# Paired context products, one claim for two turned weight tiles, and latents kept with all 128 rows

## The chip, the core and the metric

One core of a Trainium2 chip runs the whole kernel. Its engines work beside each other and meet at semaphores: PE (matrix multiply), DVE, ACT and POOL (element work), and SP, which here only issues DMAs. The time is the device time of one execution in microseconds; lower is better. The kernel before has a median of 1673.97 us over three runs (1671.38 to 1674.11). 0.2% of that, 3.3 us, is about what can be told from no change.

## What is computed

One post-norm decoder layer on 8 sequences of 256 tokens, 256 wide, all in float32:

```
x = layernorm(x + self_attention(x))
x = layernorm(x + cross_attention(x, ctx))
x = layernorm(x + mixture_of_experts(x))      # 8 experts, hidden 1024, all computed, 2 weighted
```

Self-attention has 16 heads and three branches that share the query and are mixed by a gate:

```
nq  = rms(x @ w_cq) * g_q          # 96 latent columns  -> queries
ckv = rms(x @ w_ckv) * g_kv        # 32 latent columns  -> keys and values of the latent branch
k_nope = ckv @ w_dk_nope ;  v1 = ckv @ w_dv
a1 = causal attention over the latent keys, a2 = over 64 selected tokens, a3 = causal over plain keys
out = (g0*a1 + g1*a2 + g2*a3) @ w_proj
```

Cross-attention has 16 heads of 16 columns over 256 context tokens. The experts' matrices make up most of the work.

## The kernel before

Every step is a Python generator ("thread") that yields operations. A planner, `Machine.run`, keeps a clock for each engine, picks among the threads' next operations by start time and rank, and so writes one fixed order of instructions for each engine. A low rank is preferred; the experts have rank 99 and fill what is left. A tile comes from a pool with a tag and a number of buffers; `m.claim` makes a thread wait until all the buffers it names are free, and reserves the short ones. The planner books a load as 0.6 us of issue, its bytes at 330 GB/s, one after the other, and 2.5 us to land (`commit`). None of this is visible on the chip except as the order of the instructions and the buffers that they share.

The work of a sequence `s` runs in units of four heads, `g` = 0 to 3:

- `raw` and `latents` make the 128 latent columns, 96 for the queries and 32 for keys and values. `latents` normalises the 96 in place and writes the 32 twice, side by side, into a tile `twice`. PE transposes both parts (tile `plt`), DVE scales them with the norm's gains into `lT` (rows 0 to 95) and `lk` (64 rows, the 32 rows twice).
- `latent_pairs` makes the latent keys (`kn`) and values (`vl`) for two units at a time from `lk` and the weights `wkv`. It uses 32 rows of the array for each unit, so that the two units' matmuls run beside each other on different rows. Each writes a PSUM tile of its own (`pkn`, `pvl`), which is copied out by itself.
- `project` makes queries and keys; `first` makes the scores (tile `s`, also on 32 rows each); `weighing` makes the softmax weights `pr` and `pl`.
- `products` multiplies weights by values. For this the weights must stand turned. For sequence 0, `turned` does it with PE transposes (tile `pt`) and copies. For all others the weights are parked in DRAM (`parking`: a DVE transpose and a DMA `pr<-pr`, `pl<-pl`) and loaded back in another order (DMAs `pa<-pr`, `pb<-pl`). `pa` has the tag `pt` with one buffer, `pb` the tag `pb` with one.
- `second`, `x_weighing` and `x_products` do the same for cross-attention: weights `prx`, parked and loaded as `xpt`, which also takes the one buffer of tag `pt`. In `x_products` two units share one PSUM tile `ox`: the first unit is loaded and multiplied, its buffer is given back, then the second is loaded and multiplied.
- `context` prepares keys and values of the context for all sequences at rank 60; its mask tile is `keep`. `selection` finds the 64 tokens with a row tile of tag `sc`, and `after` (the router) takes the same tag for `rT`.

A float32 matmul of 256 columns stands in the trace as two MATMUL records (two passes), and a transpose as one. The experts' tiles are `ph` (first matrix) and `py` (second).

The two lines that matter most for what follows are the products' claims:

```
for src, name, tag in (("pr", "pa", "pt"), ("pl", "pb", "pb")):
    h[name] = yield from turned(s, g, h[src], src, name, tag)
```

## Time and profile before

| | |
|---|---|
| median of three runs | 1673.97 us |
| the profiled execution, whole | 1674.96 us |
| its span, first to last instruction | 1673.2 us |
| PE busy in the span | 1609.5 us (96%) |
| DVE busy | 1158.9 us (69%) |
| ACT, POOL busy | 583.8 us, 599.7 us |
| mean granted clock of PE | 0.986 |
| DMA queue's share of the 16 engines | 57.6% |

Busy counts an engine from an instruction's start to its end. PE's matmuls overlap, so a record's mean duration (382 ns for `ph`) is longer than the distance between two starts; costs on PE are therefore read from starts. The times are from one execution, which took 1.0 us more than the median.

### The profile page before, as it was taken

To read this page: it belongs to the slowest core of one execution; us is meant where nothing else is said; L and a number is where in the kernel's file an instruction comes from. 1 tells how busy PE (TensorE), PEld (TensorE's weight loads), DVE (VectorE), ACT (ScalarE), POOL (GpSimd) and SP (SyncE) were. 2 spreads that over 40 slices of the span, in tenths; PEclk is the share of its full clock that TensorE was granted. 3 is DMA by queue.
4 is the path that set the end of the run, shared out by engine and by line. 5 is a ranking of instruction groups with operands and counts; after the bars stand their busy time and mean duration, and the time that the engine had idled before them with its cause. 6 is when DMAs were issued, how large, how long until landed. Compare 5 with 4: busy or idle time off the path is not lost.

```text
span 1673.2 us, 31920 instructions
## 1 busy us (share of the span) xinstructions
PE 1609.5 (96%) x12040; PEld 1320.2 (79%) x12040; DVE 1158.9 (69%) x2577; ACT 583.8 (35%) x2114; POOL 599.7 (36%) x795
## 2 busy tenths in 40 slices
PE   6899789999999999999999999999999999999998
PEld 4778568887887778888888688878888778888887
DVE  4968678678789874887678884688767774544333
ACT  2464543244435430434434341244435341220000
POOL 3665753253534430334235332243335332120000
PEclk8999899999999999999999999999999999999999
DMA  6311416378648675655746676566656777585552
GB/s 218 117 50 47 166 69 217 120 245 284 233 141 291 245 248 192 211 205 189 252 172 234 241 249 227 151 238 211 226 196 221 248 257 251 154 307 153 161 156 96
DMA packets 185657, 329.96 MB, mean 197 GB/s; under 512 B 13200, under 2 KB 105504, under 8 KB 178336
## 3 DMA queue, kind: packets, MB, share of 16 engines
q1 hardware_dynamic: 185504, 327.92, 57.6%
q8 instruction: 96, 1.57, 0.4%
q14 instruction: 57, 0.47, 0.1%
HBM read 237.70 MB, written 90.19 MB: 196 GB/s over the span
## 4 chain that ended last, share of the span: by engine, by line
PE 83%; issue 7%; DVE 4%; DMA 3%; POOL 1%; SPq 1%; ACT 0%; POOLq 0%; DVEq 0%; ACTq 0%
PE ph L280 23%; PE py L280 22%; PE s L280 9%; PE o L280 4%; PE pk L280 3%; PE pyo L280 3%; PE ox L280 2%; PE pv L280 2%; PE sx L280 2%; DMA xpt<-prx 1%; PE pkm L280 1%; PE pks L280 1%; PE pq L280 1%; PE pt L286 1%; PE pkr L280 1%
## 5 line engine op out<-in xcount | busy, mean ns | idle before, releaser
L280 PE MATMUL ph<-xT,w 128*128 128x256 f32 x2048 | 475.2, 382 | 3.8 <-DVE pl L98 2.6
L280 PE MATMUL py<-w,h 128*128 128x256 f32 x2048 | 471.5, 381 | 0.0
L280 PEld LDWEIGHTS ph<-xT,w 128*128 128x128 f32 x2048 | 383.8, 190 | 70.2 <-issue 16.7
L280 PEld LDWEIGHTS py<-w,h 128*128 128x128 f32 x2048 | 383.7, 190 | 59.7 <-issue 7.7
L98 ACT ACTIVATE h<-ph,b 128x256 f32<-128x256 f32 x227 | 107.5, 473 | 391.5 <-PE ph L280 340.0
L98 DVE TENSOR_SCALAR h<-ph,b 128x256 f32<-128x256 f32 x285 | 136.9, 482 | 112.5 <-PE ph L280 109.6
L98 DVE SCALAR_TENSOR_TENSOR xr<-py,rw,xr 128x256 f32<-128x256 f32 x128 | 61.2, 478 | 174.7 <-PE py L280 174.6
L98 POOL TENSOR_TENSOR prx<-prx,sumsx 128x512 f32<-128x512 f32 x128 | 130.6, 1051 | 118.8 <-DVE sumsx L98 73.2
L98 ACT ACTIVATE prx<-sx,nmx 128x256 f32<-128x256 f32 x256 | 117.0, 486 | 43.3 <-DVE nmx L98 41.9
L98 POOL TENSOR_TENSOR pr<-pr,wpr 128x256 f32<-128x256 f32 (+2 forms) x128 | 129.4, 1042 | 0.0
L98 POOL TENSOR_TENSOR rstd<-var,nhalf 128x2 f32<-128x2 f32 x24 | 17.4, 725 | 310.0 <-DVE var L98 309.9
L98 ACT ACTIVATE pl<-pl,nmpl 128x128 f32<-128x128 f32 (+1 forms) x256 | 113.1, 446 | 30.6 <-DVE nmpl L98 29.9
L98 POOL TENSOR_TENSOR kx<-turn 128x64 f32<-128x64 f32 (+1 forms) x128 | 65.3, 527 | 162.6 <-DVE turn L98 156.9
L98 ACT ACTIVATE pr<-pr,nmpr 128x128 f32<-128x128 f32 (+1 forms) x256 | 113.2, 447 | 0.0
L98 DVE TENSOR_TENSOR pr<-s,causal 128x256 f32<-128x256 f32 x128 | 74.6, 583 | 41.0 <-PE s L280 34.6
L280 PE MATMUL s<-kx,q 32*128 32x320 f32 (+1 forms) x1536 | 96.1, 390 | 0.3 <-POOL kx L98 0.3
L98 POOL TENSOR_TENSOR pl<-pl,wpl 128x512 f32<-128x512 f32 x64 | 93.1, 1475 | 2.7
L98 POOL TENSOR_TENSOR q<-turn 128x256 f32<-128x256 f32 x64 | 45.8, 735 | 134.1 <-DVE turn L98 130.8
L280 PEld LDWEIGHTS s<-kx,q 32*128 32x128 f32 x1536 | 71.2, 189 | 17.8 <-issue 7.1
L98 DVE TENSOR_REDUCE nmx<-sx 128x2 f32<-128x512 f32 x128 | 79.1, 678 | 8.5 <-PE sx L280 8.5
L98 DVE TENSOR_TENSOR pl<-s,causal 128x256 f32<-128x256 f32 x128 | 74.3, 581 | 12.6 <-PE s L280 8.6
L98 DVE TENSOR_REDUCE nmpr<-pr 128x4 f32<-128x256 f32 (+2 forms) x128 | 80.5, 673 | 0.0
(217 smaller groups left out, 2385.1 us busy)
## 6 DMA issues: line engine op xcount, KB each, us to landing
w<-in_W SPq DMA_DIRECT2D x256, 512.0 KB, 4.2
pr<-pr SPq DMA_DIRECT2D x28, 1024.0 KB, 4.1
pa<-pr SPq DMA_DIRECT2D x28, 1024.0 KB, 6.9
prx<-prx SPq DMA_DIRECT2D x28, 1024.0 KB, 5.2
xpt<-prx SPq DMA_DIRECT2D x28, 1024.0 KB, 6.5
pl<-pl SPq DMA_DIRECT2D x28, 768.0 KB, 4.9
pb<-pl SPq DMA_DIRECT2D x28, 768.0 KB, 7.2
xT<-in_xT SPq DMA_DIRECT2D x8, 256.0 KB
```

The lines of the kernel that those rows point to most:

```text
L98: return Op(self.name, us, outs, ins, lambda: getattr(self.engine, kind)(*args, **kw))
L280: lambda: nc.tensor.matmul(out, lhsT, rhs, start=start, stop=stop, skip_group_check=share > 1),
L286: return Op("PE", 0.11, [out], [in_], lambda: nc.tensor.transpose(out, in_, ident[:n, :n]), lag=0.17)
```

## The change

In words: `wkv` gets 128 rows, zero in rows 0 to 95, and is loaded by one DMA instead of four. The latents stay together: all 128 columns are normalised in place, transposed by two instructions instead of four, and scaled by one DVE instruction into `lT`; `twice`, `lk` and `gkv` go. `latent_pairs` uses all 128 rows, one matmul after the other, into one PSUM tile, which is copied out by one instruction. `turned` takes a list of one unit's two weights, or of two units' one weight, claims two buffers of the tag `pt` (which now has two) at once, and only then loads or transposes. `x_products` multiplies two units in one run. To make room, `sv` moves to the tag `turn`, and `keep` to the tag `sc`, which has one buffer.

```diff
-    wkv = fixed("wkv", [64, 2, 2, P])
-    gkv = fixed("gkv", [64, 1])
+    wkv = fixed("wkv", [P, 2 * H * VH])
...
-        for n in range(2):
-            yield dma(gkv[bass.ts(n, 32)], a["g_norm"][QL:P])
...
-        for n in range(2):
-            for v in range(2):
-                yield dma(wkv[bass.ts(n, 32), :, v], up[n, v])
+        yield dma(wkv[QL:P], a["w_up"][QL:P, 0 : 2 * H * VH])
...
     def zeros():
+        yield G.memset(wkv[0:QL], 0.0)
...
-    def turned(s, g, t, src, name, tag):
-        if by_dram(s):
-            yield seen("parked", src, s, g)
+    def turned(s, todo):
+        dst = []
+        for t, src, g in todo:
+            if by_dram(s):
+                yield seen("parked", src, s, g)
+            dst.append(two([P, t.shape[1]], "pt", "turned"))
+        yield m.claim(*dst)
+        for x, (t, src, g) in zip(dst, todo):
+            yield from turn_one(s, g, t, src, x)
+        return dst
...
-        sv = one([P, H * VH], "sv", "sv")
+        sv = two([P, H * VH], "turn", "sv")
...
-        plt = mtile([P, 2, T], "plt")
-        yield group([tr(plt[0:QL, 0, bass.ts(i, P)], lat[:, i, 0:QL]) for i in range(2)])
-        yield group([tr(plt[0:64, 1, bass.ts(i, P)], twice[:, i].rearrange("p n c -> p (n c)")) for i in range(2)])
-        m.release(lat, twice)
-        yield V.tensor_scalar(lT[0:QL], plt[0:QL, 0], gcol[0:QL], None, ALU.mult)
-        yield V.tensor_scalar(lk, plt[0:64, 1], gkv, None, ALU.mult)
+        plt = mtile([P, T], "plt")
+        yield group([tr(plt[:, bass.ts(i, P)], lat[:, i]) for i in range(2)])
+        m.release(lat)
+        yield V.tensor_scalar(lT, plt, gcol, None, ALU.mult)
...
-                ps = [mtile([P, T], "p" + name) for _ in range(2)]
...
-                        ops.append((p_, wkv[rows, g, 0], lk[rows]))
-                    else:
-                        ops += [(p_[:, bass.ts(i, P)], lk[rows, bass.ts(i, P)], wkv[rows, g, 1]) for i in range(2)]
...
-                yield group([mm(*op, share=2) for op in ops], 0.1)
-                for n, p_ in enumerate(ps):
-                    yield copied(t[:, n], p_)
+                p_ = mtile([P, 2, T], "p" + name)
+                if name == "kn":
+                    yield group([mm(p_[:, n], wkv[:, bass.ts(2 * g + n, P)], lT) for n in range(2)])
+                else:
+                    w = wkv[:, bass.ds(H * VH + 2 * P * g, 2 * P)]
+                    yield group([mm(p_[:, i], lT[:, bass.ts(i, P)], w) for i in range(2)])
+                yield copied(t, p_)
...
-                for src, name, tag in (("pr", "pa", "pt"), ("pl", "pb", "pb")):
-                    h[name] = yield from turned(s, g, h[src], src, name, tag)
+                h["pa"], h["pb"] = yield from turned(s, [(h[src], src, g) for src in ("pr", "pl")])
...
-            keep = one([P, T], "keep", "keep")
+            keep = one([P, T], "sc", "keep")
...
-                for n in range(2):
-                    pr = xa[s][g + n]["pr"]
-                    xt = yield from turned(s, g + n, pr, "prx", "xpt", "pt")
+                both = yield from turned(s, [(xa[s][g + n]["pr"], "prx", g + n) for n in range(2)])
+                xt = [parts_of(x, s).rearrange("p k h (q c) r -> p h c q k r", q=2) for x in both]
...
+                        for n in range(2)
+                        for c in range(2)
+                        for j in reversed(range(4))
...
+                m.release(*both)
```

More of the change, by code (lines that the diff above doesn't have):

```diff
@@ L404, in setup @@
         yield seen("staged", 0)
-        up = a["w_up"][QL:P, 0 : 2 * H * VH].rearrange("r (v g n c) -> n v r g c", v=2, n=2, c=P)
-        for n in range(2):
-            for v in range(2):
-                yield dma(wkv[bass.ts(n, 32), :, v], up[n, v])
+        yield dma(wkv[QL:P], a["w_up"][QL:P, 0 : 2 * H * VH])
         done.add("latent weights")
@@ L621, in parking, with turn_one @@
                 done.add(("parked", name, s, g))
-    def turned(s, g, t, src, name, tag):
-        if by_dram(s):
-            yield seen("parked", src, s, g)
+    def turned(s, todo):
[8 more added lines that the diff above has]
+        return dst
+    def turn_one(s, g, t, src, dst):
         n = t.shape[1] // (P * HG)
-        dst = one([P, HG * n * P], tag, name)
-        yield m.claim(dst)
         if by_dram(s):
@@ L643, in turned @@
             m.release(t)
-        return dst
     def weigh(t, f):
@@ L774, in latents @@
         lT = one([P, T], "lT", "lT")
-        lk = one([64, T], "lk", "lk")
-        yield m.claim(lT, lk)
+        yield m.claim(lT)
         yield seen("inputs")
-        twice = two([P, 2, 2, 32], "turn", "twice")
-        yield V.tensor_tensor(
-            lat[:, :, 0:QL], lat[:, :, 0:QL], rs[:, 0, :].unsqueeze(2).to_broadcast([P, 2, QL]), ALU.mult
-        )
-        yield V.tensor_tensor(
-            twice,
-            lat[:, :, QL:P].unsqueeze(2).to_broadcast([P, 2, 2, 32]),
-            rs[:, 1, :].unsqueeze(2).unsqueeze(3).to_broadcast([P, 2, 2, 32]),
-            ALU.mult,
-        )
-        plt = mtile([P, 2, T], "plt")
-        yield group([tr(plt[0:QL, 0, bass.ts(i, P)], lat[:, i, 0:QL]) for i in range(2)])
-        yield group([tr(plt[0:64, 1, bass.ts(i, P)], twice[:, i].rearrange("p n c -> p (n c)")) for i in range(2)])
-        m.release(lat, twice)
-        yield V.tensor_scalar(lT[0:QL], plt[0:QL, 0], gcol[0:QL], None, ALU.mult)
-        yield V.tensor_scalar(lk, plt[0:64, 1], gkv, None, ALU.mult)
+        for w, (lo, hi) in enumerate(parts):
+            yield V.tensor_tensor(
+                lat[:, :, lo:hi], lat[:, :, lo:hi], rs[:, w, :].unsqueeze(2).to_broadcast([P, 2, hi - lo]), ALU.mult
+            )
+        plt = mtile([P, T], "plt")
+        yield group([tr(plt[:, bass.ts(i, P)], lat[:, i]) for i in range(2)])
+        m.release(lat)
+        yield V.tensor_scalar(lT, plt, gcol, None, ALU.mult)
         m.release(plt)
-        d["lT"], d["lk"] = lT, lk
+        d["lT"] = lT
         done.add(("latent", s))
@@ L919, in project @@
                 m.release(pv)
-                if g == NHG - 1:
-                    m.release(d["lT"])
                 done.add(("values", s, g))
@@ L930, in latent_pairs @@
                 yield seen("heads", s, 2 * g)
-                lk = d["lk"]
+                lT = d["lT"]
                 t = one([P, 2, T], name, name)
                 d[name, g] = t
-                ps = [mtile([P, T], "p" + name) for _ in range(2)]
-                yield m.claim(t)
-                yield m.claim(*ps)
-                ops = []
-                for n, p_ in enumerate(ps):
-                    rows = bass.ts(n, 32)
-                    if name == "kn":
-                        ops.append((p_, wkv[rows, g, 0], lk[rows]))
-                    else:
-                        ops += [(p_[:, bass.ts(i, P)], lk[rows, bass.ts(i, P)], wkv[rows, g, 1]) for i in range(2)]
-                if name != "kn":
-                    ops = ops[0::2] + ops[1::2]
-                yield group([mm(*op, share=2) for op in ops], 0.1)
-                for n, p_ in enumerate(ps):
-                    yield copied(t[:, n], p_)
-                m.release(*ps)
+                p_ = mtile([P, 2, T], "p" + name)
[5 more added lines that the diff above has]
+                yield copied(t, p_)
+                m.release(p_)
                 done.add((name, s, g))
-                if name != "kn" and g == 1:
-                    yield seen("kn", s, 1)
-                    m.release(lk)
+            if name == "vl":
+                yield seen("kn", s, 1)
+                yield seen("values", s, NHG - 1)
+                m.release(lT)
     def scores(h, d, g, st, which):
@@ L1072, in products @@
                 yield seen("vl", s, g // 2)
-                vl = pro[s]["vl", g // 2][:, g % 2].rearrange("p (i c) -> p i c", i=2)
+                vl = pro[s]["vl", g // 2][:, :, bass.ts(g % 2, P)]
                 if g == 0:
@@ L1298, in x_products @@
                 o = mtile([P, T], "ox")
-                for n in range(2):
-                    pr = xa[s][g + n]["pr"]
-                    xt = yield from turned(s, g + n, pr, "prx", "xpt", "pt")
-                    turned_ = parts_of(xt, s).rearrange("p k h (q c) r -> p h c q k r", q=2)
-                    yield group(
-                        [
-                            mm(
-                                o[bass.ts(j, 32)],
-                                vx[:, c, HG * (g + n) + j, :],
-                                turned_[:, j, c],
-                                n == 0 and c == 0,
-                                n == 1 and c == 1,
-                                share=4,
-                            )
-                            for c in range(2)
-                            for j in reversed(range(4))
-                        ],
-                        0.3,
-                    )
-                    m.release(xt)
+                both = yield from turned(s, [(xa[s][g + n]["pr"], "prx", g + n) for n in range(2)])
+                xt = [parts_of(x, s).rearrange("p k h (q c) r -> p h c q k r", q=2) for x in both]
+                yield group(
+                    [
+                        mm(
+                            o[bass.ts(j, 32)],
+                            vx[:, c, HG * (g + n) + j, :],
+                            xt[n][:, j, c],
+                            n == 0 and c == 0,
+                            n == 1 and c == 1,
+                            share=4,
+                        )
+                        for n in range(2)
+                        for c in range(2)
+                        for j in reversed(range(4))
+                    ],
+                    0.3,
+                )
+                m.release(*both)
                 yield copied(oT[:, g // 2, :], o)
```

## The prediction

> **What bounds the kernel now.** I read the page's busy shares first, then the busy time by stretch, because a mean over the span hides where PE has no work:

> ```profile
> PE 1609.5 (96%) x12040; PEld 1320.2 (79%) x12040; DVE 1158.9 (69%) x2577; ACT 583.8 (35%) x2114; POOL 599.7 (36%) x795
> ```

> ```profile
> 0.00:250.00 250.00, 210.12 (x1884) 166.34 (x1884) 181.48 (x451) 118.53 (x418) 145.66 (x208) 0.92 0.33 111
> 250.00:1631.00 1381.00, 1363.86 (x9995) 1122.92 (x9995) 963.89 (x2095) 465.26 (x1696) 453.34 (x587) 1.00 0.63 216
> 1631.00:1673.20 42.20, 35.56 (x165) 30.97 (x163) 13.52 (x31) 0.00 (x0) 0.69 (x1) 0.98 0.30 99
> ```

> In each row the stretch is followed by its length and PE's busy time; the clock is third from the right. PE idles 39.9 us in the first 250, 17.1 in the next 1381 and 6.6 at the end, when the last layernorm leaves. The first `ph` starts at 250.09: until then no expert can fill PE's gaps, and the way from sequence 0 to its experts sets the pace. After it PE is the bound, and a microsecond off another engine buys nothing. So two things count: PE's own work, start to start, and the waits that the planner's order leaves on PE.

> **PE's work.** The unit comes from the chain of waits, where PE runs without a break; then three places of the timeline (start, duration, records):

> ```profile
> 1542.24 6.91 PE ph L280 x32
> ```

> ```profile
> 511.70 0.81 PE L280 MATMUL ph<-xT,w 128*128 128x256 f32 x3
> ...
> 512.44 0.70 PE L280 MATMUL pkn<-lk,wkv 32*128 32x256 f32 x4
> ...
> 513.07 1.13 PE L280 MATMUL ph<-xT,w 128*128 128x256 f32 x4
> ...
> 552.79 0.71 PE L280 MATMUL pvl<-wkv,lk 32*128 32x128 f32 x8
> 553.44 0.92 PE L280 MATMUL py<-w,h 128*128 128x256 f32 x3
> ...
> 1214.27 0.38 PE L286 MATMUL plt<-ident,lat 128*96 128x128 f32 x2
> 1214.49 1.89 PE L280 MATMUL py<-w,h 128*128 128x256 f32 x8
> ...
> 1510.67 0.81 PE L280 MATMUL ph<-xT,w 128*128 128x256 f32 x3
> 1511.41 1.07 PE L280 MATMUL ox<-xpt,vx 128*32 128x256 f32 x16
> 1512.41 0.92 PE L280 MATMUL ph<-xT,w 128*128 128x256 f32 x3
> ```

> A 256-column record on the full array takes 6.91 / 32 = 0.216 us.

> *Latent keys and values.* Three `ph` records from 511.70 should hand over at 512.35; `pkn` starts at 512.44, 0.09 late, as the array changes from full to 32 rows. It then holds PE for 0.63. Packed `pkn` costs 0.72. On the full array its four records of 256 columns cost 4 x 0.216 = 0.86: 0.14 more. `pvl` holds PE for 0.65 and, with 0.09 before it, costs 0.74; afterwards it too has four records of 256 columns: 0.13 more. Read group by group, 11 of the 16 `pkn` and 14 of the 16 `pvl` groups enter from full-array work like these. The other 7 stand beside work that is packed anyway and cost about 0.43 (`pkn` from 40.50 to 40.93); they lose about 0.45 each. Sum: 11 x 0.14 + 14 x 0.13 + 7 x 0.45 = **+6.5 us**. [...]

> *Transposes.* The two `plt` of a part hold PE for 0.22 (1214.27 to 1214.49). Four become two for each of 8 sequences: **-1.8 us**.

> *Context products.* A run of 16 `ox` records costs 1.00 and 0.09 on entry. The tile's view has the last record of this run starting at 1512.1, so a step inside is 0.69 / 15 = 0.046 us and the exit 0.31. One run of 32 costs 0.09 + 31 x 0.046 + 0.31 = 1.83 against 2 x 1.09 = 2.18: 0.35 less, 16 times, **-5.6 us**.

> PE's work in all: **-0.9 us**, which is nothing. [...]

> **The waits on PE.**

> ```profile
> PE ox L280 <- DMA xpt<-prx: 4.5, 4, 1.9
> PE o L280 <- DMA pa<-pr: 4.4, 1, 4.4
> ...
> PE ox L280 <- DVE xpt L98: 2.1, 2, 1.4
> ```

> (Total, times, longest.) *Paired context loads.* PE waited for 4 of the 28 `xpt` loads, 4.5 us. Median landing is 6.5 us after issue; the planner books 0.6 + 3.2 + 2.5 = 6.3, so it sends PE there 0.2 early. A pair is 2.1 MB. No row shows two such loads issued together. Below: fully overlapped, 6.9 after the first issue. Above: one after the other, 13.0. The nearest row is `pa` with `pb` 3.1 us behind it at 1396.87: `pb` took 7.65 against its median of 7.2, so they overlap mostly. At the 307 GB/s of the busiest slice the second MB adds 3.4: I take 9.9, where the planner books 9.5. That is as early as before, for 14 pairs in place of 28 loads: half of 4.5, **-2.2 us**. Ends: -4.5 if no pair is late; 14 x 3.5 = +49 if all land after 13.0 and nothing hides it. On SP the loads of expert weights (`w`) stand behind these; an expert is 64 records, 13.8 us of PE, and its halves are double buffered, so a delay of 3 to 6 us stays covered. No PE wait on `w` is listed.

> *Main units.* `pa` now leaves only when `pl` is parked too. Behind it on SP the same weight loads queue, and PE fills the time with experts. In the first 250 us there is no such fill: the one wait of 4.4 stands there (at 190). There `pa` went out at 187.19, after `pl` at 186.35, so the later claim changes nothing. I take 0; ends -4.4 and +11 (28 loads, 0.4 late each).

> *The first 250 us.* For sequence 0 the second unit's transposes no longer wait for the first unit's product, so the waits for `xpt` copies (2.1 by DVE, 0.4 by ACT) should go, and one DVE instruction less (`lk`, 0.47) stands ahead of the first rotation. Against this, `keep` shares `sc` with the selection: in the built order only 4 of 8 contexts come ahead of the first `ph`, 4 x 3.45 = 13.8 us of PE work moved to where PE is full. But other work of sequence 1 takes its place: priced by the starts of this trace, the instructions ahead of the first `ph` make 171 us in place of 173. I take **-1.5 us**, ends -8 (idle falls by the copy waits and the 5.2 before `ptx`) and +8 (half of the moved contexts is not replaced).

> *At no cost.* Zeroing `wkv` on POOL is like `vx` (0.95 us for 1024 columns); POOL idles 4.64 us before `sq` at 7.75. Uncovered it would be +1. Five DMA issues fewer on SP at some 0.45 bring the first weights 2.3 us forward, but PE first waits there for `lat` and the selection. Copying `kn` or `vl` at once is 0.59 on ACT where two took 0.65: beside PE. `sv` in `turn` is one tile of 5 in the whole run.

> **Sum.** -0.9 - 2.2 - 1.5 = -4.6 on the profiled execution's 1674.96 (1673.2 of span, 1.8 around it): 1670.4. The median of the runs is 1.0 lower, so **1669.5 us**, own range 1664 to 1675.

> **The rivals.**

> 1. *Late pairs, slower: 1684 us.* Place: the claim of both `pt` buffers and the two loads behind it. If the pair lands nearer 13.0 than 9.9, PE meets it 3.5 us early by the planner's clock. In the profile one load in seven was late at a deficit of 0.2; at 3.5 I take five pairs of 14, 17 us, of which experts hide nothing, PE being in order. With the 2.2 not saved and a few us kept for pairs that slip anyway: 1669.5 + 15 = 1684. It decides from (3.3 + 4.5) / 14 = 0.56 us of extra wait for a pair. For it: late `xpt` loads are already PE's costliest wait after 250 us. Against: the overlap of `pa` and `pb`.
> [...]
> 3. *A shorter start: 1663 us.* The order of sequence 0's context is tighter (no score group between `ptx` and `plg`, which took 4.86 at the slow clock): another 6.5 off.
> 4. *The claim changes nothing, 1674:* the planner's new order gives the savings back elsewhere.

> **Chances.** Forecast 0.50 (0.30 faster, 0.17 the same, 0.03 slower), rival 1 0.27 (slower 0.26, same 0.01), rival 2 0.09 (slower 0.05, same 0.04), rival 3 0.09 (faster), rival 4 0.05 (same). Faster 0.39, same 0.27, slower 0.34. No change means within 3.3 us of 1673.97, about what a measurement can tell. The range 1662 to 1686 takes in rivals 1 and 2 and leaves the far ends out.

> **What would show it.** Right: `pkn` and `pvl` with 64 records each at 0.216; `ox` in 16 runs of 1.74; PE busy within 3 us of 1609; waits of `ox` on its loads under 3 us; the first `ph` near 248. Wrong: the second load of a pair landing over 11 us after the first issue, waits on it over 8 us in sum, or PE idle over 45 in the first 250.

## The result, and the profile after

| | before | after |
|---|---|---|
| median of the runs | 1673.97 us | 1702.24 us |
| ratio, 95% interval | | 1.0176 [1.0162, 1.019] |
| profiled execution, whole / span | 1674.96 / 1673.2 us | 1704.22 / 1702.4 us |
| PE idle in the span | 63.6 us | 77.0 us |
| PE busy while its granted clock was 0.5 | 31.9 us | 70.2 us |
| PE's work, priced at full clock | 1593.6 us | 1590.3 us |

The changed kernel is 28 us slower. It lies above the range, and on the other side of the forecast.

The last row of the table is PE's busy time less half of what stood at clock 0.5, where an instruction takes twice its time (four `pq` records 2.08 us in place of 1.03, below). The span is then the sum of three terms: work, idle time, and half of the busy time at clock 0.5. For the kernel after, 1590.3 + 77.0 + 35.1 = 1702.4. Against before that is -3.3 of work, +13.4 of idle time and +19.2 of halved clock: +29.2 us, the whole difference of the spans.

The first two views of the kernel after are the page's busy shares and the busy time by stretch (length, PE busy; the clock is third from the right):

```profile
PE 1625.4 (95%) x11960; PEld 1342.0 (79%) x11960; DVE 1180.5 (69%) x2596; ACT 569.0 (33%) x2053; POOL 604.5 (36%) x798
```

```profile
0.00:250.00 250.00, 204.85 (x1886) 162.48 (x1886) 189.02 (x469) 112.64 (x388) 135.38 (x195) 0.91 0.32 102
250.00:1659.00 1409.00, 1383.61 (x9904) 1147.37 (x9905) 977.08 (x2096) 456.33 (x1666) 468.44 (x603) 0.98 0.63 213
1659.00:1702.40 43.40, 36.95 (x172) 32.19 (x170) 14.37 (x33) 0.00 (x0) 0.70 (x1) 0.98 0.32 103
```

PE has 80 records fewer and is busy 15.9 us longer. More busy time with less work is the sign of a slower clock. The middle stretch shows it: its clock was 1.00 before and is 0.98 now. From the first `ph` on the clock stood at 0.5 for 44.1 us in place of 4.8, and 17.2 of the 19.2 us of halved clock are lost there.

Where the clock goes can be seen around one wait. First the kernel after in the timeline of PE (start, duration, records, idle time before and its releaser), then the busy time by stretch around it:

```profile
937.04 0.81 PE L280 MATMUL s<-lx,q 32*128 32x128 f32 x4
943.13 1.92 PE L280 MATMUL s<-lx,q 32*128 32x128 f32 x11 [5.29 <-ACT prx L98]
...
948.18 2.08 PE L280 MATMUL pq<-lT,wq 96*128 96x256 f32 x4
```

```profile
930.00:939.80 9.80, 7.84 (x97) 6.40 (x95) 9.24 (x19) 4.04 (x18) 7.22 (x10) 1.00 0.70 275
939.80:956.88 17.08, 13.62 (x73) 9.91 (x74) 15.63 (x36) 6.25 (x25) 5.87 (x7) 0.50 0.54 182
956.88:966.00 9.12, 9.12 (x66) 7.09 (x65) 7.22 (x12) 5.18 (x22) 2.25 (x3) 1.00 0.61 177
```

PE stands 5.29 us because the score tile that it wants is still being read by ACT, which had itself waited 4.42 us for POOL (`prx`). While it stands, the clock goes to 0.5 and stays there for 17.08 us. The four `pq` records at 948.18 take 2.08 where the same row takes 1.03 at 84.04. Of these 17.08 us PE was busy for 13.62, so 6.8 us of work were lost behind a wait of 5.3. The wait cost 12.1.

The waits on PE of the kernel after (total, times, longest):

```profile
PE ppos L286 <- DVE sc L98: 13.1, 3, 7.7
PE o L280 <- DMA turned<-pr: 8.2, 3, 4.0
PE ppos L286 <- DVE gm L98: 8.0, 2, 6.6
PE ptx L286 <- DVE xr L98: 7.7, 3, 4.2
PE pl L280 <- DMA wA<-in_w_gi: 5.6, 1, 5.6
PE s L280 <- ACT prx L98: 5.3, 1, 5.3
```

The paired context loads (`turned<-prx` before `ox`) are not in this list: PE never waited for one. The transpose of the selection's row (`ppos`) stands at 21.1 us in place of 9.3, the main units' loads (`o`) at 10.5 in place of 4.6, `s` at 6.1 in place of 0.3. (`ptx` is the transpose of a layer's output.) The waits are of many kinds and in many places.

### The profile page after: what moved, and what is told of

Same layout as the page of the kernel before. It is cut to its first block, busy times and chain, and to the rows that moved or that the text cites. A ratio compares the mean times of both kernels' runs of the same rounds, so it can differ in the third digit from the quotient of the medians.

```text
span 1702.4 us, 31755 instructions
## 1 busy us (share of the span) xinstructions
PE 1625.4 (95%) x11960; PEld 1342.0 (79%) x11960; DVE 1180.5 (69%) x2596; ACT 569.0 (33%) x2053; POOL 604.5 (36%) x798
## 4 chain that ended last, share of the span: by engine, by line
PE 79%; DVE 8%; issue 7%; DMA 3%; POOL 2%; ACT 0%; SPq 0%; POOLq 0%; DVEq 0%; ACTq 0%
PE ph L280 21%; PE py L280 21%; PE s L280 8%; PE o L280 3%; PE pk L280 3%; PE pyo L280 2%; PE pv L280 2%; PE pq L280 2%; PE ox L280 2%; PE sx L280 2%; PE pks L280 1%; DMA turned<-pl 1%; PE pkm L280 1%; PE pt L286 1%; DVE pr L98 1%
## 5 line engine op out<-in xcount | busy, mean ns | idle before, releaser
L280 PE MATMUL ph<-xT,w 128*128 128x256 f32 x2048 | 477.1, 383 | 0.5 <-DVE pl L98 0.5
L280 PE MATMUL py<-w,h 128*128 128x256 f32 x2048 | 469.5, 382 | 0.9 <-DMA w<-in_W 0.9
L280 PEld LDWEIGHTS ph<-xT,w 128*128 128x128 f32 x2048 | 385.7, 191 | 64.1 <-issue 7.3
L280 PEld LDWEIGHTS py<-w,h 128*128 128x128 f32 x2048 | 388.6, 191 | 60.3 <-issue 5.8
L98 DVE TENSOR_SCALAR h<-ph,b 128x256 f32<-128x256 f32 x331 | 158.9, 482 | 133.7 <-PE ph L280 130.8
L98 ACT ACTIVATE h<-ph,b 128x256 f32<-128x256 f32 x181 | 85.9, 475 | 338.8 <-PE ph L280 299.2
L98 POOL TENSOR_TENSOR prx<-prx,sumsx 128x512 f32<-128x512 f32 x128 | 130.4, 1050 | 158.6 <-DVE sumsx L98 91.2
L98 DVE SCALAR_TENSOR_TENSOR xr<-py,rw,xr 128x256 f32<-128x256 f32 x128 | 61.2, 478 | 165.6 <-PE py L280 165.2
L98 ACT ACTIVATE prx<-sx,nmx 128x256 f32<-128x256 f32 x256 | 117.3, 488 | 97.3 <-DVE nmx L98 77.8
L98 POOL TENSOR_TENSOR kx<-turn 128x64 f32<-128x64 f32 (+1 forms) x128 | 66.4, 538 | 188.3 <-DVE turn L98 184.0
L98 POOL TENSOR_TENSOR pr<-pr,wpr 128x256 f32<-128x256 f32 (+2 forms) x128 | 130.1, 1047 | 0.0
L98 POOL TENSOR_TENSOR rstd<-var,nhalf 128x2 f32<-128x2 f32 x24 | 17.3, 723 | 316.0 <-DVE var L98 315.7
L98 ACT ACTIVATE pl<-pl,nmpl 128x128 f32<-128x128 f32 (+1 forms) x256 | 113.5, 450 | 21.6 <-POOL q L98 11.4
L98 ACT ACTIVATE pr<-pr,nmpr 128x128 f32<-128x128 f32 (+1 forms) x256 | 113.5, 450 | 0.0
L98 DVE TENSOR_TENSOR pr<-s,causal 128x256 f32<-128x256 f32 x128 | 74.9, 586 | 49.8 <-PE s L280 47.3
L98 POOL TENSOR_TENSOR q<-turn 128x256 f32<-128x256 f32 x64 | 46.8, 748 | 152.6 <-DVE turn L98 152.6
L98 POOL TENSOR_TENSOR pl<-pl,wpl 128x512 f32<-128x512 f32 x64 | 92.9, 1473 | 2.7
L280 PE MATMUL s<-kx,q 32*128 32x192 f32 (+1 forms) x1536 | 92.7, 383 | 0.0
L280 PEld LDWEIGHTS s<-kx,q 32*128 32x128 f32 x1536 | 68.1, 185 | 18.7 <-issue 6.5
L98 DVE TENSOR_REDUCE nmx<-sx 128x2 f32<-128x512 f32 x128 | 79.1, 679 | 3.5 <-PE sx L280 3.4
L98 DVE TENSOR_REDUCE nmpr<-pr 128x4 f32<-128x256 f32 (+2 forms) x128 | 80.6, 674 | 0.0
L98 DVE TENSOR_TENSOR pl<-s,causal 128x256 f32<-128x256 f32 x128 | 74.0, 578 | 4.7 <-PE s L280 4.2
```

What stands on the lines that cost most here:

```text
L98: return Op(self.name, us, outs, ins, lambda: getattr(self.engine, kind)(*args, **kw))
L280: lambda: nc.tensor.matmul(out, lhsT, rhs, start=start, stop=stop, skip_group_check=share > 1),
```

## The experiments

Each kernel ran beside the kernel before on the same chip. The columns "work", "idle" and "at 0.5" are those of the first table, from one profiled execution each; "span" is that execution's. For e13 this execution was 6.8 us under the median, for e15 5.0 above.

| | median | ratio to before [95%] | span | work | idle | at 0.5 |
|---|---|---|---|---|---|---|
| e1 `keep` in `sc` alone | 1694.86 | 1.0133 [1.0113, 1.0152] | 1693.9 | 1592.0 | 74.2 | 55.4 |
| e2 latents alone | 1695.28 | 1.0127 [1.0111, 1.0144] | 1695.2 | 1597.5 | 72.3 | 51.0 |
| e3 pairs alone | 1671.70 | 0.999 [0.9979, 1.0001] | 1669.4 | 1592.2 | 57.8 | 38.8 |
| e4 before, long waits added | 1725.85 | 1.0309 [1.0292, 1.0327] | 1725.7 | 1595.3 | 99.4 | 61.8 |
| e8 before, short waits added | 1699.59 | 1.0155 [1.0124, 1.0186] | 1698.6 | 1596.6 | 76.1 | 51.9 |
| e5 before, lag 0.25 | 1694.54 | 1.0123 [1.0103, 1.0143] | 1691.5 | 1589.4 | 76.1 | 52.1 |
| e6 before, lag 0.10 | 1693.42 | 1.012 [1.0099, 1.0142] | 1689.7 | 1590.2 | 73.7 | 51.6 |
| e9 after, lag 0.25 | 1725.54 | 1.0301 [1.026, 1.0342] | 1723.3 | 1592.5 | 90.5 | 80.7 |
| e10 after, lag 0.10 | 1712.64 | 1.0249 [1.0217, 1.0281] | 1708.3 | 1593.8 | 85.4 | 58.4 |
| e7 after, `keep` elsewhere | 1696.02 | 1.0126 [1.0099, 1.0154] | 1693.4 | 1591.0 | 74.0 | 56.7 |
| e13 the same, lag 0.25 | 1692.54 | 1.012 [1.0101, 1.0139] | 1683.9 | 1593.5 | 68.0 | 44.8 |
| e14 the same, lag 0.10 | 1695.00 | 1.0129 [1.0108, 1.015] | 1692.7 | 1593.7 | 71.8 | 54.4 |
| e15 e1, lag 0.25 | 1703.82 | 1.0181 [1.0164, 1.0198] | 1707.0 | 1586.5 | 82.9 | 75.1 |
| e11 before, slack 2 | 1688.78 | 1.0097 [1.0073, 1.0121] | 1684.7 | 1593.3 | 66.3 | 50.4 |
| e12 after, slack 2 | 1685.24 | 1.0067 [1.0043, 1.0091] | 1684.2 | 1598.9 | 60.8 | 49.0 |
| e16 pairs alone, slack 2 | 1679.93 | 1.0043 [1.0026, 1.0061] | 1679.5 | 1587.5 | 62.5 | 59.1 |
| e17 e7, slack 2 | 1696.28 | 1.0138 [1.0117, 1.0158] | 1695.4 | 1591.0 | 77.4 | 53.8 |
| e18 pairs alone, slack 1 | 1688.84 | 1.0089 [1.007, 1.0109] | 1684.5 | 1585.7 | 73.0 | 51.5 |

Read down the column "work": in all 18 it lies between 1585.7 and 1598.9. The times lie 54 us apart. What tells these kernels apart is mostly idle time and clock. The figure is rough: one kernel under two plans differs by up to 8.6 us in it (after, 1590.3; e12, 1598.9), so a few us of work are not settled by it.

**The change in parts (e1, e2, e3).** Three kernels from the kernel before, each with one part. e1:

```diff
-            keep = one([P, T], "keep", "keep")
+            keep = one([P, T], "sc", "keep")
```

> The kernel before with one edit: the mask tile `keep` takes the one buffer of tag `sc`. No work changes. If the shared buffer is the cause (selection late, PE waiting at `ppos`), most of the loss is here: 1690 to 1700 us, waits of `ppos` on DVE rise from 9 to about 20 us. If the pairs or the latents are the cause: 1674 within 3. If any new order of the planner's costs about as much: anywhere from 1674 to 1695, with waits at places that have nothing to do with `sc`.

e2 has the hunks of `wkv`, `latents` and `latent_pairs`, e3 those of `turned`, `products` and `x_products`. Both need the room that `sv` gives up:

```diff
-        sv = one([P, H * VH], "sv", "sv")
+        sv = two([P, H * VH], "turn", "sv")
```

> The kernel before with the full-row latents alone (and `sv` in tag `turn`, for space). By the sum of the prediction PE's work rises by 6.5 - 1.8 = 4.7 us: 1679. If the latents are the cause of the loss: 1695 or more. If any new order costs: 1679 plus up to 20, with the waits and the halved clock to show for it.

> The kernel before with the paired context products and the claim of two `pt` buffers alone (and `sv` in `turn`). By the sum PE's work falls by 5.6 us: 1668. If the paired claim is the cause (loads issued together land late): 1690 or more with over 10 us of PE waits on the `turned` loads. If any new order costs: 1668 plus up to 20, waits elsewhere.

The pairs alone cost nothing: 1671.7, not told apart from before. PE's waits at `o` for the main units' loads are 4.9 us there, as before (4.6), although the claim is the changed one. The other two cost 21 to 22 us each, and do not add up: after is 28 us slower, not 43. In e2 the work rose by 3.9 us, near the 4.7 of the prediction's sum (6.5 less 1.8), and the other 18 of the span are idle time and clock. In e1 nothing is computed differently at all. The waits of e2 on PE:

```profile
PE o L280 <- ACT prx L98: 7.5, 1, 7.5
PE ppos L286 <- DVE gm L98: 6.7, 1, 6.7
PE ox L280 <- DMA xpt<-prx: 6.5, 3, 3.1
...
PE o L280 <- DMA pb<-pl: 5.7, 1, 5.7
```

None of the four is a wait on latents. `ox`, which e2 does not touch, waits longer than before, and the longest ends when ACT is done with a score tile (`prx`). This pointed away from the parts and to the order of everything.

**The price of a wait, with the order held (e4, e8).** The kernel before in its own order. At one expert of each sequence, 16 (e8: 6) chained copies on ACT and a matmul that reads their tile stand ahead of a group of `ph`. The matmul's result is overwritten, and the order of the rest stays. ACT has the copies to do besides its own work:

```diff
+            for _ in range(16):
+                nc.scalar.copy(probe, probe)
+            nc.tensor.matmul(ph[:, 0:P], probe, probe, start=True, stop=True)
...
+                    if e == 4 and c == 4:
+                        now.issue = behind(now.issue, ph)
```

> The kernel before, its order kept, with 8 added waits of PE, one in each sequence's experts (expert 4, chunk 4): 16 chained ACT copies of 0.27 us, about 4.4 us, then a small matmul that reads their result. If a wait costs its own length alone: 8 x 4.4 = 35, so 1709 us. If the halved clock behind it counts as in the changed kernel (half of one to two windows of 3.4 us of work lost for each): 8 x (4.4 + 1.7 to 3.4) = 49 to 62, so 1723 to 1736, and the clock's rows show 8 windows more at 0.5.

> The kernel before with 8 added waits of PE as in the long ones, but of 6 ACT copies, about 1.6 us and 2.5 with what surrounds them. The 8 long ones cost 52 us, 6.5 each. If the clock halves only behind a wait of some 3 us or more: 8 x 2.5 = 20, so 1694, with no more windows at 0.5 than before. If any wait halves it: 8 x (2.5 + 1.7) = 34, so 1707.

PE's timeline at the fourth sequence, in e4 and then in e8:

```profile
775.74 3.40 PE L280 MATMUL ph<-xT,w 128*128 128x256 f32 x15
784.86 0.79 PE L1393 MATMUL ph<-probe 128*128 128x128 f32 x2 [5.72 <-ACT probe L1392]
785.45 6.08 PE L280 MATMUL ph<-xT,w 128*128 128x256 f32 x16
```

```profile
771.74 2.97 PE L280 MATMUL ph<-xT,w 128*128 128x256 f32 x13
777.10 0.49 PE L1393 MATMUL ph<-probe 128*128 128x128 f32 x2 [2.40 <-ACT probe L1392]
777.43 5.31 PE L280 MATMUL ph<-xT,w 128*128 128x256 f32 x16
```

Sixteen `ph` records should take 16 x 0.216 = 3.46 us. Behind the long wait they take 6.08, behind the short one 5.31. The stretch behind the long wait, by stretches:

```profile
783.60:790.43 6.83, 5.57 (x14) 4.59 (x15) 2.03 (x8) 1.33 (x5) 0.00 (x0) 0.50 0.00 1
790.43:985.00 194.57, 190.98 (x1521) 156.71 (x1520) 150.06 (x307) 79.75 (x293) 76.77 (x98) 1.00 0.62 213
```

In e4 six of the eight waits can be seen (4.05 to 5.78 us; those of the first two sequences are hidden), each with 3.41 or 6.83 us at clock 0.5. The kernel is 52.3 us slower than the kernel before beside it, nearly 9 for each wait of 5.4 in the mean. By the terms of the span this is 35.8 of idle time, 15.0 of clock and 1.7 of work. The first case expected of e8, that only waits of some 3 us and more halve the clock, was wrong. In e8 the waits were one of 1.71 and four of 2.40 to 2.46, and 3.41 us at clock 0.5 followed the first four of these five; only the last, at 1384, had none. (A sixth wait was 0.69.) So a wait of 2.4 us cost up to 1.7 us (half of 3.41) more than its length, and its length alone does not decide whether it does.

```profile
774.96:778.37 3.41, 1.27 (x7) 1.17 (x8) 0.16 (x1) 1.93 (x7) 0.00 (x0) 1.00 0.58 206
778.37:781.78 3.41, 3.41 (x10) 2.66 (x9) 2.14 (x8) 0.22 (x1) 0.00 (x0) 0.50 0.02 5
...
1379.12:1382.53 3.41, 2.73 (x13) 2.07 (x11) 2.66 (x8) 1.52 (x4) 0.00 (x0) 1.00 1.03 331
1382.53:1385.94 3.41, 1.62 (x9) 1.47 (x10) 3.31 (x13) 1.80 (x7) 1.62 (x5) 1.00 1.01 415
1385.94:1389.36 3.42, 3.42 (x54) 2.66 (x53) 1.64 (x3) 0.71 (x2) 0.10 (x1) 1.00 0.81 306
```

Why the half clock sometimes stays on is not shown: of 214 windows at half clock with PE busy for over 95%, 34 were followed by another.

In the kernels before and after the granted clock is 0.5 or 1.00 and nothing between, and its stretches at 0.5 are 3.41, 6.83, 10.24, 13.65 and, once, 17.08 us long (the last of each kernel, 3.37 and 3.48, aside). What sets the grid and the clock was not shown. Had each wait cost its length alone, e8 would have cost 12.1 us in all. It cost 25.0 (25.4 by the spans: 12.5 of idle time, 10.0 of clock and 3.0 of work). Of the clock at most 4 x 3.41 / 2 = 6.8 stands behind the added waits; the rest is behind waits that the kernel had already, where the half-clock stretches came out longer.

**The order alone (e5, e6, e9, e10).** The planner books 0.17 us of `lag` after a matmul before others may read it. One constant is altered, for the kernel before and for the one after. The same operations then come in another order (and some copies on another engine, since the planner picks that too):

```diff
-lag=0.17
+lag=0.25
```

and 0.10 in e6 and e10.

> The kernel before; the planner alone is told that a matmul's result comes 0.25 us after its end in place of 0.17. No instruction is added or taken away, only the order differs. If the order alone can cost what the changed kernel lost: 1680 to 1700 us, PE's work at the full clock stays at 1593 within 3, and the difference is idle time and PE's time at half clock. If the planner's order is robust and the parts of the change have causes of their own: 1674 within 3.

> The same with 0.10 us in place of 0.17. Order theory: again 1675 to 1700, and not the same waits as with 0.25. Own-cause theory: 1674 within 3.

> The changed kernel with the planner's lag at 0.25 in place of 0.17. The kernel before went from 1674 to 1694.5 with this edit. If the change's own effect is near nothing and its loss is the order: 1690 to 1705 here, on either side of the changed kernel's 1702, and work at the full clock 1590 within 3. If the change costs something by itself: 1702 or more, as much above 1694.5 as the changed kernel is above 1674.

> The changed kernel with the lag at 0.10. The kernel before went to 1693.4 with it. Order theory: 1690 to 1705. Own-cost theory: 1715 to 1725.

The kernel before loses 20.0 and 18.8 us, with no operation added, removed or resized, and with 3 to 4 us less of PE's work in the profile. A new order is worth as much as most of what the change lost. The waits of e5:

```profile
PE ppos L286 <- DVE gm L98: 11.9, 3, 6.9
PE o L280 <- DMA pb<-pl: 8.2, 2, 6.9
PE ppos L286 <- DVE sc L98: 8.0, 2, 7.4
PE ptx L286 <- DVE xr L98: 6.3, 4, 3.5
```

They are much like those of the kernel after: `ppos` behind the selection, `o` behind a main unit's load, `ptx`.

After, too, lost by both lags, 23 and 10 us, and here the order theory missed: it had put e9 and e10 at 1690 to 1705, and they took 1725.5 and 1712.6. Lag against lag, the changed kernel is slower than the kernel before by 28.3 us (0.17), 31.0 (0.25) and 19.2 (0.10). So a lost order is not the whole of it; something in the change costs at each of these lags. And 0.17 is the best of three for both kernels. It may describe the chip better than the other two values, and then they are not neutral; no run tells that from luck. What does not rest on it are e2 above and e7 below, which kept 0.17 and took 1695.3 and 1696.0.

The order also tells e3 from the rest. Compared group by group, PE's order in e3 is that of before up to 208 us, the first `ox`, where the edit begins. e1 leaves it at 61 us, e5 at 53, e6 at 36, e2 and after at 13. Of these, only the kernel that keeps the start is not slower. (In e2 and after the edit itself begins there.)

**The shared tag (e7, e13, e14, e15).** In the kernel after, `keep` goes into a tag of eight buffers, so that no selection waits for a context mask:

```diff
-            keep = one([P, T], "sc", "keep")
+            keep = eight([P, T], "h", "keep")
```

e13 and e14 are this with lag 0.25 and 0.10; e15 is e1 with lag 0.25.

> The changed kernel with one edit: `keep` takes a buffer of tag `h` (eight of them, idle while the contexts are made) and not the one of `sc`. If sharing `sc` is what the change lost by: 1675 to 1682, what is left being the latents' work. If the order is the cause: 1685 to 1710 with other waits.

> The changed kernel with `keep` in tag `h` and the lag at 0.25. With `sc` shared it took 1725.5, the kernel before 1694.5. If the shared buffer makes the difference: 1690 to 1700. If the rest of the change does: 1715 or more. If neither and each order is a draw: anything from 1690 to 1725, and not the same way in the next run.

> The same with the lag at 0.10. With `sc` shared it took 1712.6, the kernel before 1693.4. Shared buffer: 1690 to 1700. Rest of the change: 1708 or more.

> The kernel before with `keep` in `sc` alone and the lag at 0.25. Without the sharing this lag took 1694.5. If the shared buffer costs by itself: 1705 to 1725, with `ppos` waits over 20 us. If not: 1690 to 1700.

Without the shared tag the changed kernel takes 1696.0, 1692.5 and 1695.0 at three lags. The reordered kernel before takes 1694.5 and 1693.4. At the lags 0.25 and 0.10 the change without its shared tag is as fast as the kernel before (within 2.0 us), as the sum of PE's work said. At 0.17 it is 22 us slower.

With the tag shared it is slower by 6.2, 33.0 and 17.6 us at the same three lags, and the kernel before by 9.3 (e15 against e5; e1's 21 us at 0.17 have the lost order in them too). All point one way. The place can be seen in the stretch ahead of the first `ph` (length, PE busy), for e7 and then for the kernel after:

```profile
0.00:254.34 254.34, 217.27 (x1954) 172.46 (x1955) 192.61 (x480) 119.64 (x410) 142.73 (x206) 0.93 0.34 110
```

```profile
0.00:255.51 255.51, 207.36 (x1898) 164.66 (x1899) 194.00 (x481) 118.11 (x413) 135.81 (x195) 0.91 0.31 100
```

PE idles 37.1 us there without the shared tag and 48.2 with it. In the five pairs of kernels that differ in the tag alone and have no slack, the tag adds 6.8 to 14.3 us of this idle time (37.1 to 45.4 without, 48.2 to 58.3 with). The contexts, which can fill PE's gaps there, go with it. Without the shared tag all 8 of them are made ahead of the first `ph` (6 in e5), with it 4 to 6, because each mask then waits for a buffer that the selections and the router use too. The idle time need not show at `ppos`: in e15 I expected over 20 us there and found 6.9, while the transposes `pt` waited 15.9 us for POOL, against 4.6 in e5.

With slack 2, below, the shared tag is 11 us faster (e12, e17). There 7 contexts come ahead of the first `ph`, and the idle time ahead of it is 39.5 us with the tag and 44.5 without. So the tag seems to cost by the contexts that it keeps back, and a plan that keeps back only one does not pay. This fits all six pairs, but no run moved the contexts alone, and the price for the whole kernel varies with the plan.

**Slack in the plan (e11, e12, e16, e17, e18).** If the waits come from a plan that sends PE to each result at the last moment, planning PE later than the result should cure them. In `Machine.start`, for what PE reads from other engines:

```diff
-            t = max(t, at + (0.0 if eng == op.engine else 0.15))
+            t = max(t, at + (0.0 if eng == op.engine else 2.0 if op.engine == "PE" else 0.15))
```

(1.0 in e18.)

> The kernel before; the planner takes what another engine writes for PE as ready 2.0 us after its planned end, not 0.15, so that PE is sent there later and fills with other work. If the waits come from a planner that sends PE too tightly: idle after the first `ph` falls from 23.8 to under 12 us, no halved clock there, though the first part gets longer by some us: 1665 to 1680. If the waits come from lateness of more than 2 us: as the other new orders, 1690 to 1700.

> The changed kernel with the same 2.0 us. If tight planning is the cause: the loss goes, within 5 us of the kernel before with the same slack, 1665 to 1680. If the change's own waits (pairs of loads, one `sc`) are the cause: still 15 us or more above it.

> Pairs alone (`keep` in a tag of its own, packed latents) with the slack of 2.0 us. The kernel before with this slack took 1688.8. By PE's work the pairs are worth -5.6: 1683. If order decides: 1670 to 1695.

> The changed kernel with `keep` in tag `h` and the slack of 2.0 us. The whole change with this slack took 1685.2, the kernel before 1688.8. If the shared buffer still costs with slack: 1675 to 1680. If slack hides it: 1685 within 4.

> Pairs alone with a slack of 1.0 us. With none it took 1671.7, with 2.0 us 1679.9. If slack shortens the waits steadily: under 1670, better than both kernels. If each order is a draw: 1675 to 1695.

After gained 17 us by it and before lost 15; the pairs lost 8 and 17, and e7 stood still. In e11 PE idled 25.8 us after the first `ph`, where I had expected under 12 and where the kernel before has 23.8. e17 missed both of its ranges. Slack of this kind is one more reordering, not a cure. No kernel tried beats both: the nearest is e3, whose interval includes no difference.

## Why the prediction was wrong

**PE's work, -0.9: right within what can be told.** The profile has -3.3, and mere reorderings move this figure by as much (e5: -4.2). Inside it, the groups of `pkn` and `pvl` are as priced. In the timeline of the kernel after, `pkn` holds PE from 349.10 to 350.05, 0.95 us, of which 0.09 is the change to 32 rows behind it and 0.86 the four records, as foreseen:

```profile
349.10 1.03 PE L280 MATMUL pkn<-lT,wkv 128*128 128x256 f32 x4
350.05 2.87 PE L280 MATMUL s<-kx,q 32*128 32x192 f32 x48
...
582.03 1.93 PE L280 MATMUL ox<-turned,vx 128*32 128x256 f32 x32
583.90 1.13 PE L280 MATMUL ph<-xT,w 128*128 128x256 f32 x4
```

A run of 32 `ox` holds PE for 1.87, not 1.74: the pairs save 0.22 each in place of 0.35, 3.5 us in place of 5.6. It is a small miss. The step of 0.046 was a mean over records that start in fours, about 0.216 us apart (at 1511.41, 1511.65, 1511.86 and 1512.08 in the kernel before), so 16 more records add 4 x 0.216 = 0.86 and not 16 x 0.046 = 0.74. Rival 2, that all 32 groups lose what packing saves beside packed work, falls: from the 0.86 us of a full-array group and the 0.43 of a packed one beside packed work that is 32 x 0.43 = 13.8 us, an estimate, or 12 less the transposes, and e2's work rose by 3.9. That margin is no wider than the scatter of the figure; the better witness are the groups, of which all 32 in e2 hold PE for 0.86 to 0.97 us, as priced.

**The paired context loads, -2.2: right in sign, too small.** PE waited for no pair; the 4.5 us of waits for loads went, and so did those for copies. (When the pairs landed is not in the trace.) Rival 1, late pairs, which had the best chance of all rivals, is refuted by the list of waits and by e3.

**The main units, 0: right for what it priced.** In e3, with the same claim, PE waits for these loads as before (4.9 us, 4.6 before). So the 10.5 of the kernel after are not the claim's alone; they came in its new order.

**The first 250 us, -1.5: wrong; this is the step that failed in its own terms.** The prediction saw that only 4 of 8 contexts would come ahead of the first `ph`, and that is what happened. Then it let other work of sequence 1 take their place, and took PE's idle time to fall. The other work came in part (PE's work up to the first `ph`, at full clock, fell from 195.8 to 191.0 us, where 2 less were foreseen), but it did not fill the gaps: the idle time up to there rose by 8.3 us, and the first `ph` starts at 255.5 and not near 248. With `keep` elsewhere (e7) that idle time is 37.1 us, less than before (39.9), so this step failed at the shared tag. One of the prediction's own signs of being wrong, PE idle for over 45 us in the first 250, came true with 45.15.

**All other waits, at nothing: wrong too.** The part on the waits foresaw -3.7 in all. Measured are +13.4 of idle time, of which 5.1 lie behind the first `ph`. The prediction costed the waits that the edit touches and took all others to stay. In a kernel whose order a planner writes, every wait is drawn again. e5 and e6 show what this draw is worth with no operation edited: 12.5 and 10.1 us of idle time.

**What was never a term: the clock.** +19.2 us, the largest of the three, and put at nothing without a reason. The cue stood in the rows that the prediction quotes, 0.92, 1.00 and 0.98. The kernel before has 31.9 us of busy time at clock 0.5, 28.9 of it ahead of the first `ph`. Of these, 20.2 stand behind waits of 6.7, 4.4 and 5.2 us, the rest behind waits of 2.7 us and less. Behind the first `ph` its longest wait is 1.9, and only 3.0 us of its busy time were at half clock. The kernel after has 37.4 there. With the clock as a term, a wait of 5 us is priced at about 9 (e4).

**Rival 4**, the planner gives the savings back elsewhere, had part of the mechanism. It was priced at 1674 because it was thought to give back only what was gained. It is not bounded by the gain. The kernel before stands in a favourable order, 15 to 20 us ahead of the same kernel under three other plans (e5, e6, e11), and the prediction took that order as a property of the kernel. An edit that shuffles the plan is to be forecast near 1694, plus its own effect. e2 fell there, and so did e7, the change without its shared tag; e3, which kept the order of the first 208 us, did not.

Together: 22 of the 28 us lie between the kernel before and the change without its shared tag (e7). Its work is the same, and e5 and e6 lose about as much by a new order alone, so I put these down to the order. The other 6 are the shared tag (after against e7). At the lags 0.25 and 0.10 the order is a new one on both sides, and the tag's 33 and 18 us are as good as the whole difference.

What stays open: how much of the tag's price is its own and how much one more draw, since a shared buffer also makes a new order; whether 0.17 is lucky or right; and whether e3's 1671.7 is a saving or an order kept. More orders of each kernel would tell, and were not tried.

## What to carry to other kernels

When a greedy plan writes the order, compare an edit with its kernel over several plans that differ in one constant of the planner; one plan against one measures the draw with the edit. Split a span into work at full clock, idle time and halved clock before looking for a cause: here the work stayed within 13 us over twenty kernels. Price a wait on a busy PE at its length and about half of the stretch at half clock behind it: here up to 1.7 us for each 3.41 us window, of which at least one followed wherever PE was left idle for over 2.05 us of a window at full clock (156 of 156). Before a buffer is shared, ask what work fills the gaps of the bottleneck and whether it needs that buffer.

## What the hardware showed unexpectedly

The wait of 2.40 us behind which the clock halves, and the 17.08 us at half clock behind one wait of 5.29 with PE 80% busy, are told above. One thing more: DVE's scan and POOL's multiplications took longer in some places where they stood beside each other, 2.27 us in place of 0.68 and 4.77 in place of 4.03. In the kernel after, the selection's last steps stand beside a multiplication on POOL, and PE waits 7.74 us for them. DVE's timeline, then POOL's:

```profile
88.33 0.72 DVE L98 TENSOR_TENSOR left<-left,sc 1x256 f32<-1x256 f32 x1
89.09 2.27 DVE L98 TENSOR_TENSOR_SCAN sc<-left 1x256 f32<-1x256 f32 x1
91.39 0.65 DVE L98 TENSOR_TENSOR sc<-sc,left 1x256 f32<-1x256 f32 x1
```

```profile
87.74 4.77 POOL L98 TENSOR_TENSOR pr<-pr,wpr 128x512 f32<-128x512 f32 x4
```

The scan takes 0.68 in the median of its eight times in the kernel after, and here 2.27. Of the 16 scans of the two kernels, before and after, the five that took 1.02 to 2.27 all stand beside POOL's work on two tensors (four beside multiplications, one beside the subtraction and addition that make `kx`); the other eleven took 0.63 to 0.68, nine of them with POOL at rest. POOL's four multiplications take 4.77 here and 4.03 in the median of the kernel before. This is read from the overlap alone; the cause is not shown, and no run took it apart.
